# The evidence products of the first pair: from halves of 64 contexts two at a time to quarters of 32 contexts four at a time

## The chip, the cores and the metric

The kernel runs on one core of a Trainium2 chip. A core has TensorE for matrix products (PE in the profile, and PEld for its loads of the stationary operand), VectorE (DVE), ScalarE (ACT), GpSimd (POOL) and SyncE (SP, which here issues transfers). The metric is the device time in microseconds of one execution, median of several runs.

## The reference, cut to what matters

Eight sequences of 512 tokens with 256 features. Each token attends to 64 contexts of its sequence, and the result, the evidence, enters every layer that follows beside the normalised token.

```
nx = layer_norm(x)                                # (8, 512, 256)
scores = (nx @ Wq) @ (prototype_bank @ Wk).T * H ** -0.5
weights = softmax(scores)                         # over 64 contexts
evidence = weights @ (prototype_bank @ Wv)
combined = concat([nx, evidence, anchor])         # (8, 512, 768)
h = silu(combined @ e_w1 + e_b1)                  # three experts of 512
expert_out = h @ e_w2 + e_b2
routed = sum(expert_out * router_probs)           # over the experts
g = sigmoid(silu(combined @ gate_w1 + gate_b1) @ gate_w2 + gate_b2)
out = x + g * (routed @ out_w + out_b)
```

## The kernel before, in words

The sequences are taken in four pairs, j = 0 to 3, all in fp32. Features lie on the 128 partitions and the 512 tokens of one sequence along the free dimension. The evidence itself is never formed. The context values are multiplied by the weights first (`S["vw", j]`, one half of 64 partitions for each sequence of the pair), and a layer adds the product of these values (stationary, 64 partitions by 128 columns) with the softmax weights (`S["wT", j]`, moving, 64 partitions by 512 tokens) to what the nx products of that layer left in a bank of PSUM. These are the evidence products. In the trace and in the order they read `<-wT,vw`.

The first layer works on chunks of 128 output features, two chunks to a group. Group 0 is the gate, groups 1 to 6 are the three experts with two groups each. In one group seven nx products, in a scheme that saves the eighth, go to three banks: U, Y and Z (`U[n]`, `Y[n]`, `Z[n]`, tiles ps_u, ps_y, ps_z). Between products, ACT copies the bank (`keep_part`) and DVE adds the later ones (`add`, L1074 to L1076). A bank is used again by the next group, with the tile framework's semaphores keeping order. For the first pair (j = 0) the order of PE's work is that of the calls in `gate_layer` and `expert_layer`. Each engine takes its instructions in the order of the program.

For the first pair there are four blocks of evidence products, all from the function `evidence`:

- block 1, at the end of `gate_layer`: eight products, for Y0, Z0, U0 and a fourth bank W of group 0, and for the fresh banks Y and Z of groups 1 and 2;
- blocks 2 and 3, at the ends of the first and the second expert: eight products each, U and Z of the two groups that are ending, Y and Z of the two groups that follow;
- block 4, at the end of the third expert: four products, U and Z of groups 5 and 6.

Products of the two sequences alternate, so that one uses rows 0 to 63 of TensorE's array and the next rows 64 to 127. A product appears in the trace as two matmul records and two weight loads, called passes here.

After block 1 DVE adds Y0, Z0 and W to what was kept, then makes `T` (fourth combination of the pair's x, L675), which the product U0 of the next layer reads as its moving operand. After block 2 ACT applies two silus to U1 and U2, copies a weight sum (`v_F`, L909), and computes two standard deviations of the next pair (L584). DVE takes their reciprocals (L590), normalises x of the next pair in eight instructions (L594), adds Y3, and transposes a block of second-layer weights (L515), which PE multiplies next (`ps_w2o`, L523).

For the later pairs (j = 1 to 3) `half_layers` follows a table of 57 slots written by hand. There every product is made in two halves of 64 rows by `half_product`, two to a slot. When the half before it in the same bank ran on other rows of the array, `half_product` lets TensorE's queue wait on a semaphore until that one has ended. `read_bank` forgets what went before in a bank.

Of the kernel before, what the change touches and what calls it, by code (L numbers as in the profile page):

```python
# [16 lines left out]
def kernel(  # L17
# [52 lines left out]
    P = 128  # L70
    B, T, H = x.shape
    CT = context.shape[1]
# [55 lines left out]
    TB = 32  # L128
# [55 lines left out]
    rows = scr[:, P : 2 * P]  # L184
# [375 lines left out]
    S = {}  # L560
# [256 lines left out]
    def values(j, c=0):  # L817

        return S["vw", j] if j < 2 or c >= NE else w1[:, KH + j - 2, :]
# [190 lines left out]
    def product(ps, lhsT, rhs, start=False):  # L1010

        return nc.tensor.matmul(ps, lhsT, rhs, start=start, stop=True, skip_group_check=not start)  # L1012

    def half_product(ps, lhsT, rhs, half, start=False):

        prior_half, prior = last_half.get(ps.name, (half, None))
        if prior_half == half or start:  # L1020
            ins = product(ps, lhsT, rhs, start)
        else:
            tag = bank_of[ps.name]
            if tag not in finished:
                finished[tag] = [tc.alloc_semaphore(f"half_{tag}"), 0]
            finished[tag][1] += 1
            prior.then_inc(finished[tag][0])
            group = f"half_{tag}_{finished[tag][1]}"
            tc.add_to_no_dep_group(group, prior.ins)
            tc.no_tile_sem_insts.add(prior.ins.name)  # L1030
            nc.tensor.wait_ge(*finished[tag])
            ins = product(ps, lhsT, rhs, start)
            tc.declare_fence(ins.ins, group=group)
        last_half[ps.name] = half, ins

    def read_bank(ps):
        last_half.pop(ps.name, None)
# [6 lines left out]
    def evidence(j, groups, W=None):  # L1044

        todo = []
        for n, new in groups:
            c = 2 * GROUPS[n]  # L1050
            for i, ps in ((0, Y[n] if new else U[n]), (1, Z[n])):
                todo.append((ps, i, c + (i if new else 1 - i), new))
        if W is not None:
            c = 2 * GROUPS[0]
            todo[:0] = [(Y[0], 0, c, False), (Z[0], 1, c, False)]
            todo[4:4] = [(U[0], 0, c + 1, False), (W, 1, c + 1, True)]
        for ps, i, c, start in todo:
            half = slice(i * CT, (i + 1) * CT)
            product(ps, values(j, c)[half, c * P : (c + 1) * P], S["wT", j][half, :], start=start)

    def chunk(n, i, d):
        if n == 0:
# [66 lines left out]
    def gate_layer(j, steps):  # L1129
# [29 lines left out]
        W = bank(1, f"ps_w_{j}")  # L1159
        fresh(j, 0)  # L1160
        evidence(j, [(m, True) for m in PAIRS[0]], W=W)

        add(n, 0, 0, Y[n])
# [15 lines left out]
    def expert_layer(j, e, steps):  # L1179
# [62 lines left out]
        if e + 1 < E:  # L1242
            fresh(j, e + 1)
            evidence(j, [(m, False) for m in (a, b)] + [(m, True) for m in PAIRS[e + 1]])
        else:
            evidence(j, [(m, False) for m in (a, b)])
# [387 lines left out]
    with tc.manual_schedule(engines=None):  # L1634
# [5 lines left out]
        for d in range(2):  # L1640
            half = slice(d * NX // 2, (d + 1) * NX // 2)
# [187 lines left out]
```

## Time and profile before

| | us |
|---|---|
| median of three runs | 455.45 (455.0 to 455.94) |
| the profiled execution | 455.56 |
| its span on the core | 453.7 |
| PE busy | 449.2 |
| DVE busy | 367.2 |
| ACT busy | 216.6 |
| POOL busy | 115.8 |

The span runs from the first to the last instruction of the core; 1.86 us of the profiled execution lie around it. Matmuls are pipelined and their ends are modelled, so two passes in a row overlap in the records. The distance between their starts, not their duration, is the time that a pass takes.

### The profile page before, as it was taken

To read this page: it belongs to the slowest core of one execution; us is meant where nothing else is said; L and a number is where in the kernel's file an instruction comes from. 1 tells how busy PE (TensorE), PEld (TensorE's weight loads), DVE (VectorE), ACT (ScalarE), POOL (GpSimd) and SP (SyncE) were. 2 spreads that over 40 slices of the span, in tenths; PEclk is the share of its full clock that TensorE was granted. 3 is DMA by queue.
4 is the path that set the end of the run, shared out by engine and by line. 5 is a ranking of instruction groups with operands and counts; after the bars stand their busy time and mean duration, and the time that the engine had idled before them with its cause. 6 is when DMAs were issued, how large, how long until landed. Compare 5 with 4: busy or idle time off the path is not lost.

```text
span 453.7 us, 5398 instructions
## 1 busy us (share of the span) xinstructions
PE 449.2 (99%) x1707; PEld 213.4 (47%) x1707; DVE 367.2 (81%) x687; ACT 216.6 (48%) x382; POOL 115.8 (26%) x176
## 2 busy tenths in 40 slices
PE   9999999999999999999999999999999999999996
PEld 8644556444444444444444444444444444444445
DVE  4889989668969999857979999777979838678983
ACT  3445685539332257547440276658240356557000
POOL 6558767531242130000243220000151300000020
PEclk9999999999999999999999999999999999999999
DMA  8999698665641567710203158401103381000014
GB/s 256 382 175 188 110 257 165 103 115 105 57 77 28 117 155 172 139 42 7 43 5 45 26 165 167 65 0 30 24 0 46 47 213 22 0 0 1 0 20 74
DMA packets 122124, 41.34 MB, mean 91 GB/s; under 512 B 106452, under 2 KB 115472, under 8 KB 121584
## 3 DMA queue, kind: packets, MB, share of 16 engines
q1 hardware_dynamic: 117184, 29.25, 32.2%
q0 software_dynamic: 4624, 11.63, 10.8%
q8 instruction: 13, 0.21, 0.2%
q14 instruction: 15, 0.12, 0.1%
q10 hardware_dynamic: 288, 0.13, 0.1%
HBM read 31.23 MB, written 7.39 MB: 85 GB/s over the span
## 4 chain that ended last, share of the span: by engine, by line
PE 99%; DVE 0%; issue 0%
PE ps_u L1012 45%; PE ps_z L1012 20%; PE ps_y L1012 14%; PE ps_gu L1012 3%; PE ps_vc L1012 3%; PE ps_w2o L523 2%; PE ps_vw L806 2%; PE ps_s L684 2%; PE ps_gz L1012 2%; PE ps_tokens L1012 1%; PE ps_v L359 1%; PE ps_m L359 1%; PE ps_gy L1012 1%; PE ps_wake L312 1%; PE ps_kq L373 0%; PE ps_ar L462 0%
## 5 line engine op out<-in xcount | busy, mean ns | idle before, releaser
L1012 PE MATMUL ps_u<-nxT,w 64*128 64x512 f32 (+1 forms) x184 | 87.4, 594 | 0.0
L1127 DVE TENSOR_TENSOR h<-h,pb 128x512 f32<-128x512 f32 x96 | 63.1, 694 | 15.9 <-ACT h L1070 11.0
L1012 PE MATMUL ps_u<-h,w2o 128*128 128x512 f32 x144 | 63.9, 593 | 0.0
L1070 ACT ACTIVATE h<-h,abias 128x512 f32<-128x512 f32 x72 | 49.0, 717 | 26.5 <-DVE h L1076 26.2
L1539 POOL TENSOR_TENSOR yb<-yb,xb 128x512 f32<-128x512 f32 x14 | 20.2, 1443 | 129.2 <-DVE yb L1538 115.0
L1012 PE MATMUL ps_z<-T,ws 64*128 64x512 f32 (+1 forms) x92 | 46.4, 590 | 0.0
L1012 PE MATMUL ps_z<-nxT,ws 64*128 64x512 f32 (+1 forms) x92 | 46.0, 591 | 0.0
L1012 PEld LDWEIGHTS ps_u<-nxT,w 64*128 64x128 f32 (+1 forms) x184 | 32.7, 187 | 27.7 <-issue 22.1
L1012 PE MATMUL ps_y<-nxT,w 64*128 64x512 f32 (+1 forms) x92 | 45.5, 590 | 0.0
L1012 PEld LDWEIGHTS ps_u<-h,w2o 128*128 128x128 f32 x144 | 27.3, 190 | 33.3 <-issue 32.1
L1012 PE MATMUL ps_u<-T,ws 64*128 64x512 f32 (+1 forms) x92 | 42.9, 590 | 0.0
L1012 PE MATMUL ps_u<-T,w 64*128 64x512 f32 (+1 forms) x98 | 42.6, 592 | 0.0
L1012 PE MATMUL ps_z<-h,w2s 128*128 128x512 f32 x96 | 42.5, 592 | 0.0
L1079 ACT COPY h<-ps_u 128x512 f32<-128x512 f32 x48 | 27.8, 580 | 17.4 <-PE ps_u L1012 17.4
L437 POOL DMA_DIRECT2D vrd<-vw x8 | 5.0, 632 | 111.2 <-ACT vw L813 111.2
L1506 DVE TENSOR_TENSOR h<-h,h 128x1024 f32<-128x1024 f32 x24 | 30.7, 1333 | 0.0
L1012 PEld LDWEIGHTS ps_z<-h,w2s 128*128 128x128 f32 x96 | 18.2, 190 | 23.0 <-issue 22.2
L1012 PE MATMUL ps_z<-wT,vw 64*128 64x512 f32 x56 | 27.5, 596 | 0.0
L1076 DVE TENSOR_TENSOR h<-h,ps_u 128x512 f32<-128x512 f32 x24 | 16.1, 684 | 10.3 <-PE ps_u L1012 10.3
L1012 PE MATMUL ps_z<-wT,w 64*128 64x512 f32 x48 | 24.1, 589 | 0.0
L1012 PEld LDWEIGHTS ps_z<-T,ws 64*128 64x128 f32 (+1 forms) x92 | 17.3, 188 | 13.2 <-issue 12.2
L1012 PEld LDWEIGHTS ps_y<-nxT,w 64*128 64x128 f32 (+1 forms) x92 | 17.3, 188 | 13.2 <-issue 12.5
(277 smaller groups left out, 889.7 us busy)
## 6 DMA issues: line engine op xcount, KB each, us to landing
pb<-pd POOLq DMA_DIRECT2D x4, 1536.0 KB, 6.5
xb<-in_x_dram SPq DMA_DIRECT2D x64, 64.0 KB, 2.6
x<-in_x_dram SPq DMA_DIRECT2D x28, 128.0 KB, 3.3
out_dram<-yb SPq DMA_DIRECT2D x56, 64.0 KB, 2.0
w<-in_L_xcond_e_w_dram SPq DMA_DIRECT2D x6, 512.0 KB, 9.4
xd<-x SPq DMA_DIRECT2D x24, 128.0 KB, 2.5
xg<-xd SPq DMA_DIRECT2D x48, 64.0 KB, 2.6
scr_wa<-in_L_xcond_e_w_dram SPq DMA_DIRECT2D x3, 512.0 KB, 17.6
```

Of the source, the lines that this page charges most:

```text
L359: nc.tensor.matmul(part(ps, h), w_sb[:, k, m * P : (m + 1) * P], part(src[:, k, :], h), start=(k == 0 and h == 0), stop=(k == KH - 1), ski ...
L437: nc.gpsimd.dma_start(S["vrd", j][i].rearrange("e c -> c e"), S["vw", j][row_half(i), R0:])
L523: nc.tensor.matmul(ps[:, d * H : (d + 1) * H], w2T[:, k, (i + d) * P : (i + d + 1) * P], ow_sb[:, k, :], start=(k == 0), stop=(k == KH - 1),)
L684: nc.tensor.matmul(ps[side(i, h), g * NH : (g + 1) * NH], mr[:, k, 2 * j + i, g * TB : (g + 1) * TB], S["nxT", 2 * j + i][:, k, h * NH : ( ...
L806: nc.tensor.matmul(ps, vT[:, k, j * 2 * CT : (j + 1) * 2 * CT], w1[:, KH + k, n0:n1], start=(k == 0), stop=(k == KH - 1),)
L1012: return nc.tensor.matmul(ps, lhsT, rhs, start=start, stop=True, skip_group_check=not start)
L1070: nc.scalar.activation(h, h if src is None else src, AF.Silu, bias=abias[:, c, 2 * j + i : 2 * j + i + 1])
L1076: nc.vector.tensor_tensor(h, h, part, ALU.add)
L1079: nc.scalar.copy(chunk(n, i, d), part)
L1127: nc.vector.tensor_tensor(h, h, S["pb", j][:, i, :, 2 * q // RC, :], ALU.mult)
L1506: nc.vector.tensor_tensor(d, p, m, ALU.subtract)
L1539: nc.gpsimd.tensor_tensor(yb, yb, S["xb", 2 * j + row][:, i, :], ALU.add)
```

## The change

`evidence` makes each product in two parts of 32 contexts. The products of the first and of the second sequence are listed apart (`first`, `second`). Two of each are taken together: their four banks get one quarter product each, on rows 0 to 31, 32 to 63, 64 to 95 and 96 to 127 of the array. This is called a quad here. The first round (s = 0) goes over all such fours, and the second round (s = 1) goes over them again with the two quarters of each sequence exchanged, so that each bank gets its other 32 contexts. All go through `half_product`, so a second-round product waits on a semaphore for the first-round product of its bank.

```
-        for ps, i, c, start in todo:
-            half = slice(i * CT, (i + 1) * CT)
-            product(ps, values(j, c)[half, c * P : (c + 1) * P], S["wT", j][half, :], start=start)
+        for ps, *_ in todo:
+            read_bank(ps)
+        first, second = ([t for t in todo if t[1] == i] for i in range(2))
+        turns = [(p, s) for s in range(2) for p in range(0, len(first), 2)]
+        for p, s in turns:
+            four = [side_[p + (r ^ s)] for side_ in (first, second) for r in range(2)]
+            for q, (ps, i, c, start) in enumerate(four):
+                rows = slice(q * TB, (q + 1) * TB)
+                half_product(
+                    ps, values(j, c)[rows, c * P : (c + 1) * P], S["wT", j][rows, :], q,
+                    start and not s,
+                )
```

TensorE's order in block 1 before (`ps_y_1` is the bank Y of group 1, the last number is the tile's; the last two rows are the first products of the next layer):

```order
L1012 MATMUL ps_y_0_407<-wT_380,vw_278 128x512
L1012 MATMUL ps_z_0_406<-wT_380,vw_278 128x512
L1012 MATMUL ps_y_1_431<-wT_380,vw_278 128x512
L1012 MATMUL ps_z_1_432<-wT_380,vw_278 128x512
L1012 MATMUL ps_u_0_405<-wT_380,vw_278 128x512
L1012 MATMUL ps_w_430<-wT_380,vw_278 128x512
L1012 MATMUL ps_y_2_433<-wT_380,vw_278 128x512
L1012 MATMUL ps_z_2_434<-wT_380,vw_278 128x512
L1012 MATMUL ps_u_1_465<-nxT_263,w_95 128x512
L1012 MATMUL ps_u_0_405<-T_322,w_95 128x512
```

Here Y0 and Z0 are complete after the first two products and W after the sixth. The same place in the change, from the last two products of the first round on, with the semaphore that each waits for:

```order
L1012 MATMUL ps_w_430<-wT_380,vw_278 128x512
L1012 MATMUL ps_z_2_434<-wT_380,vw_278 128x512
L1012 MATMUL ps_y_1_431<-wT_380,vw_278 128x512 [waits half_4]
L1012 MATMUL ps_y_0_407<-wT_380,vw_278 128x512 [waits half_3]
L1012 MATMUL ps_z_1_432<-wT_380,vw_278 128x512 [waits half_5]
L1012 MATMUL ps_z_0_406<-wT_380,vw_278 128x512 [waits half_2]
L1012 MATMUL ps_y_2_433<-wT_380,vw_278 128x512 [waits half_6]
L1012 MATMUL ps_u_0_405<-wT_380,vw_278 128x512 [waits half_0]
L1012 MATMUL ps_z_2_434<-wT_380,vw_278 128x512 [waits half_7]
L1012 MATMUL ps_w_430<-wT_380,vw_278 128x512 [waits half_1]
L1012 MATMUL ps_u_1_481<-nxT_263,w_95 128x512 [waits DMAHW6_49,DVE_49]
L1012 MATMUL ps_u_0_405<-T_322,w_95 128x512 [waits DVE_49]
```

Y0 and Z0 are now complete in the third of four quads, W in the fourth, and six quarter products stand ahead of these rows. The order of DVE, ACT and POOL is unchanged.

TensorE's order in block 4 before, from the last nx product on:

```order
L1012 MATMUL ps_u_6_882<-T_322,w_95 128x512 [waits DVE_49]
L1012 MATMUL ps_u_5_879<-wT_380,vw_278 128x512
L1012 MATMUL ps_z_5_859<-wT_380,vw_278 128x512
L1012 MATMUL ps_u_6_882<-wT_380,vw_278 128x512
L1012 MATMUL ps_z_6_861<-wT_380,vw_278 128x512
```

And in the change:

```order
L1012 MATMUL ps_u_5_927<-wT_380,vw_278 128x512
L1012 MATMUL ps_u_6_930<-wT_380,vw_278 128x512
L1012 MATMUL ps_z_5_891<-wT_380,vw_278 128x512
L1012 MATMUL ps_z_6_893<-wT_380,vw_278 128x512
L1012 MATMUL ps_u_6_930<-wT_380,vw_278 128x512 [waits half_1]
L1012 MATMUL ps_u_5_927<-wT_380,vw_278 128x512 [waits half_3]
L1012 MATMUL ps_z_6_893<-wT_380,vw_278 128x512 [waits half_7]
L1012 MATMUL ps_z_5_891<-wT_380,vw_278 128x512 [waits half_5]
```

The second round of this block follows the first at once, with no other quad between them.

## Rows read from the trace of the kernel before

**Rows 1.** The page: the span and each engine's busy time.

```profile
span 453.7 us, 5398 instructions
...
PE 449.2 (99%) x1707; PEld 213.4 (47%) x1707; DVE 367.2 (81%) x687; ACT 216.6 (48%) x382; POOL 115.8 (26%) x176
```

**Rows 2.** The waits of TensorE in the whole span: total us, times, longest.

```profile
PE ps_wake L312 <- PEq L1815: 0.8, 1, 0.8
```

**Rows 3.** Timeline of block 1: start us, us, engine, line, operation, [idle before <-releaser].

```profile
29.95 0.69 PE L1012 MATMUL ps_y<-wT,vw 64*128 64x512 f32 x1
30.06 0.69 DVE L1076 TENSOR_TENSOR hg<-hg,ps_u 128x512 f32<-128x512 f32 x1 [0.21 <-PE ps_u L1012]
30.48 0.59 PE L1012 MATMUL ps_y<-wT,vw 64*128 64x512 f32 x1
31.11 0.69 DVE L1076 TENSOR_TENSOR hg<-hg,ps_y 128x512 f32<-128x512 f32 x1 [0.37 <-PE ps_z L1012]
32.20 0.59 PE L1012 MATMUL ps_u<-wT,vw 64*128 64x512 f32 x1
32.84 0.69 DVE L1076 TENSOR_TENSOR hg<-hg,ps_w 128x512 f32<-128x512 f32 x1 [0.45 <-PE ps_w L1012]
33.06 0.59 PE L1012 MATMUL ps_y<-wT,vw 64*128 64x512 f32 x1
33.45 0.80 DVE L675 TENSOR_TENSOR T<-nxT,T 128x512 f32<-128x512 f32 x1
34.30 0.44 PEld L1012 LDWEIGHTS ps_u<-T,w 128*128 128x128 f32 x2 [0.42 <-DVE T L675]
34.55 1.02 PE L1012 MATMUL ps_u<-T,w 128*128 128x512 f32 x2
35.41 1.02 PE L1012 MATMUL ps_u<-nxT,w 128*128 128x512 f32 x2
```

**Rows 4.** Timeline of block 2 and what follows, all engines.

```profile
54.42 0.69 ACT L1070 ACTIVATE h<-ps_u,abias 128x512 f32<-128x512 f32 x1 [2.18 <-PE ps_z L1012]
55.51 0.59 PE L1012 MATMUL ps_y<-wT,vw 64*128 64x512 f32 x1
55.86 0.61 ACT L909 COPY v_F<-v_F 128x512 f32<-128x512 f32 x1
56.89 1.98 PE L1012 MATMUL ps_u<-nxT,w 128*128 128x512 f32 x4
58.12 0.18 DVE L590 RECIPROCAL rstd<-sd 128x4 f32<-128x4 f32 x1 [1.96 <-ACT sd L584]
60.41 1.66 POOL L842 TENSOR_TENSOR v_a<-vT 128x384 f32<-128x384 f32 x1
60.49 1.74 DVE L594 TENSOR_SCALAR x<-x,mv,rstd 128x256 f32<-128x256 f32 x1
62.35 1.88 DVE L594 TENSOR_SCALAR x<-x,mv,rstd 128x256 f32<-128x256 f32 x4
64.74 1.29 DVE L515 STREAM_TRANSPOSE scr_w2T<-scr_w 128x512 f32<-128x512 f32 x2
66.08 2.89 PEld L523 LDWEIGHTS ps_w2o<-ow_sb,scr_w2T 128*128 128x128 f32 x14 [0.23 <-DVE scr_w2T L515]
```

**Rows 5.** Timeline after block 3, DVE.

```profile
88.24 0.69 DVE L1127 TENSOR_TENSOR h<-h,pb 128x512 f32<-128x512 f32 x1 [1.74 <-ACT h L1070]
```

**Rows 6.** Timeline after block 4, ACT.

```profile
101.99 0.59 ACT L885 COPY vw<-ps_vc 128x512 f32<-128x512 f32 x1 [4.10 <-PE ps_vc L1012]
```

**Rows 7.** Timeline of the first pair's scores, TensorE, and the instruction after them.

```profile
18.75 2.05 PE L684 MATMUL ps_s<-nxT,mr 128*32 128x256 f32 x32
20.48 0.76 PE L462 MATMUL ps_ar<-scr_wa,condT 128*32 128x128 f32 x16
```

**Rows 8.** Timeline of TensorE: first of pair 1's 57 slots, first product behind them.

```profile
157.42 0.69 PE L1012 MATMUL ps_y<-wT,vw 64*128 64x512 f32 x1
206.68 1.12 PE L1012 MATMUL ps_gu<-hg,gw_sb 128*128 128x512 f32 x2
```

## The prediction

> **What bounds the kernel now.** I read the page first. TensorE is busy for 449.2 of 453.7 us, the next engine, DVE, for 81% [rows 1]. Busy time alone proves little where ends are modelled, so I turned to the list of waits: TensorE's matmuls stood still for nothing but 0.8 us at the start [rows 2]. Then I read the timeline around the four blocks for the distance between starts. From 32.20 to 33.06 us lie two passes [rows 3], 0.43 us each, and a full-array product takes the same 0.86 us (34.55 to 35.41, [rows 3]). So TensorE bounds the kernel, nearly without gaps, and whatever holds it up in the first 105 us is lost at the end. Nothing later waits for an idle TensorE that could take the loss up.
>
> The reader should see two more things in these rows. The half-row products already run side by side: the first passes of block 1 start at 29.95 and the last at 33.06 [rows 3], which is seven distances of 0.43 us and a slower first one, so eight steps for the sixteen passes of eight products. The array is full already. And several followers are only just in time: the weight load of U0's product is released by T and starts at 34.30, 0.25 us ahead of a matmul that starts without a gap [rows 3], and the load for `ps_w2o` at 66.08 is 0.23 us late because of DVE's transposes [rows 4].
>
> **What the change does to TensorE itself.** Before, 28 products in pairs make 14 times 2 passes. After, 56 quarter products in quads make 14 times 2 passes again. If four run at once, the passes cost 28 times 0.43 = 12.0 us in both. The gain is nothing. Four row quarters at once are shown nowhere in this trace. The nearest row is the scores, where four products on different columns of the array run at once: 32 records from 18.75 until the next instruction at 20.48 [rows 7], that is 8 quads of 0.216 us for 256 columns, half of 0.43 us. So four tiles at once keep full pace there, and I take full pace here. The bound on the other side, two at a time as before, is 12.0 us more; a milder one, 0.53 us for every quad's pass (a block's first pass now, as worked out below), is 28 times 0.10 = 2.8 us. Entry into a block costs something already. The first pass takes 30.48 - 29.95 = 0.53 us instead of 0.43 [rows 3], and four loads instead of two may add 0 to 0.1 us per block, of which I take nothing.
>
> The Trainium skill, TensorE: Matmul & The Clock Gate, section Measured speedup vs the span model, states 3.07 times, not 4, for four row tiles of 32. By it, as an estimate, a quad's pass would take 4 / 3.07 times 0.43 = 0.56 us, the 28 passes 3.6 us more, and the kernel 462.1 us. No row here shows four row tiles; the scores' four column tiles lose no such share.
>
> **The waits of the second round.** Each second-round product stands behind a semaphore. In blocks 1 to 3 a whole quad (0.86 us) lies between a product and its predecessor. Pair 1 has the same waits: its 57 slots run from 157.42 to 206.68 [rows 8], 49.26 us, against 57 times 0.86 = 49.0. I cost these at nothing, since at least one slot lies between there too. In block 4 nothing lies between. The wait ends only when the predecessor has left the array; its modelled duration is 0.59 us [rows 3], 0.16 beyond the 0.43 at which the next pass would start. With the semaphore and the loads that queue behind it, 0.2 to 0.6 us; I take **0.4 us**. ACT has been idle for 4.10 us until 101.99 [rows 6], so nobody behind block 4 is late.
>
> **Block 1: results come later.** DVE starts an add 0.63 us after the start of the bank's last pass (32.20 to 32.84, and 30.48 to 31.11 [rows 3]). Before, Y0 was ready after the second pass; after, its last pass is the sixth. That is where U0's and W's second pass stands now, at 32.20 [rows 3]. The fifth product in the queue is now U0, which waits for DVE's add of the old U0, 30.06 to 30.75 [rows 3]; the third pass was due at 30.91, so its loads come some 0.1 us late. So Y0's add starts at about 32.93. Z0's add, W's and T follow at the distance of 0.61 us seen from 32.84 to 33.45 [rows 3]: T starts at 34.76 and takes 0.80, until 35.56. The load follows 0.05 us after T (34.25 to 34.30), so U0's product starts at 35.6 instead of 34.55, and after an idle stretch its first pass takes 0.53. The next product starts at 36.57 instead of 35.41: **1.15 us**, between 0.9 (no late loads, no slow first pass) and 1.4. The new order also lets U1's product of the next layer wait for Y0's add, since it takes its bank; that wait lies inside the other one. DVE, ACT and TensorE are from here on late by the same amount, so no second loss follows.
>
> **Block 2: two hand-offs.** Before, U1 was ready after the second pass of the block and U2 after the fourth. After, both end with the sixth pass, at 55.51 [rows 4], so the two silus start at 56.14 instead of 54.42 and end at about 57.5. U3's first product takes U1's bank; the first silu ends at 56.83, about when that product was due (56.89 [rows 4]), so 0 to 0.2 us there. The longer way is through ACT: behind the silus stand the copy at 55.86, a table load and the deviations (sd), for which DVE idles 1.96 us until 58.12 [rows 4]. The copy now starts at 57.4, 1.55 us late, and DVE's reciprocal comes at about 59.7. Behind it stand eight normalisations, the add of Y3, and the two transposes at 64.74, for which `ps_w2o` waits already [rows 4]. There is no slack, so TensorE loses what DVE is late by then. It may make up a part: one normalisation took 1.74 us at 60.49 beside a POOL addition that began at 60.41, while four later ones took 1.88 together [rows 4], 0.47 each. After the shift, the first normalisations meet POOL instead of the third and fourth. If one more slips in ahead of POOL's long addition, DVE recovers 0.5 us; if none, little. **1.4 us**, between 0.9 and 1.7, U3's wait included, as it lies inside the same lateness.
>
> **Block 3.** The same lateness of 1.5 us meets DVE with 1.74 us of idle time until 88.24 [rows 5], and ACT with none of the next pair's deviations. What is left is the bank of U5, again about when it was due: **0.05 us**, 0 to 0.3.
>
> **The sum.** 1.15 + 1.4 + 0.05 + 0.4 = 3.0 us; ends together 2.0 and 4.0. Against the profiled execution (455.56: the span of 453.7 and 1.86 around it) this gives 458.6. The median is 455.45, so I say **458.5 us**, its own range 457.4 to 459.7. About 0.2%, 0.9 us, is what a measurement of this kernel tells from no change.
>
> **The rivals.**
> - *Four at a time don't keep pace.* Quarter products of different rows write to four banks at once, which no row shows; the scores of rows 7 write to one. With two at a time 12.0 us come on top (470.5), with 0.53 us for a pass 2.8 (461.3). For it: no row of this form exists. Against it: scores, and pairs, at full pace. 12%.
> - *The hand-offs are absorbed.* If DVE's order gave U0's T and the transposes in time, only block 4 and scraps of entries remain: 0.4 to 1.5 us, 455.9 to 457. For it only POOL's slow-down of the normalisations, which touches one hand-off of two. 13%.
> - *Faster: a quad's pass is shorter than 0.43 us.* A pass over 512 columns might be bound by the rows that one product uses. At half, 0.215, the four blocks would lose 6.0 us, Y0 would be ready earlier than now's W, and the time would be 450. The point from which it decides is 3.0 us on 28 passes, a pass of 0.32 us. Against it: passes of 64 rows and of 128 rows have the same distance of 0.43 [rows 3]. 5%.
> - *Forecast as summed:* 70%.
>
> **How the numbers follow.** 458.5 is the forecast's own. The range goes from 456.3, which takes in half of the absorbed case, to 462, which takes in the milder form of the first rival (461.3); outside lie some 5% of faster, 6% below 456.3 otherwise and 6% above. Slower: the forecast, the first rival, and a small part of the absorbed case, together 0.86. Within 0.2% (up to 456.4): most of the rest of that case, 0.08. Faster: 0.06.
>
> **What would show it.** In the changed trace: quads whose four records start within some 0.03 us and whose passes are 0.43 us apart; DVE's T at about 34.8, the product that reads it at about 35.6 behind an idle gap of 0.5 to 1 us; the deviations 1.55 us later against block 2, and a gap ahead of `ps_w2o`; a gap of 0.2 to 0.6 between the two rounds of block 4. The prediction is wrong if passes of quads are not 0.43 us, if the semaphore waits cost in blocks 1 to 3 too, or if the gaps at U0 and `ps_w2o` are missing.

## The result and the profile after

The changed kernel takes 458.38 us (median of 4 runs, 457.94 to 459.01) against 455.56 us before (median of 4, 455.0 to 455.94). The ratio is 1.0064 with an interval of [1.0047, 1.0081], so it is 2.8 us slower. The prediction was 458.5 us, in a range of 456.3 to 462. The profiled execution took 459.01 us.

The page of the changed kernel, span and busy times, to be read against [rows 1]:

```profile
span 457.2 us, 5520 instructions
...
PE 450.9 (99%) x1763; PEld 217.2 (48%) x1763; DVE 365.8 (80%) x687; ACT 216.3 (47%) x382; POOL 115.0 (25%) x176
```

TensorE has 56 passes and 56 weight loads more (28 products became 56) and the whole program 122 instructions more. The span grew by 3.5 us, and TensorE's busy time by 1.7. The rest is in new waits, which the list of TensorE's waits names (total us, times, longest; before, only the first row was there [rows 2]):

```profile
PE ps_wake L312 <- PEq L1824: 0.8, 1, 0.8
PE ps_u L1012 <- DVE T L675: 0.7, 1, 0.7
PE ps_u L1012 <- DVE h L1085: 0.5, 1, 0.5
PE ps_w2o L523 <- ACT h L1079: 0.5, 1, 0.5
```

The second row is block 1, the fourth is the stretch behind block 2. The third is neither. It lies in pair 3, and the prediction had nothing there.

Of the 3.5 us, 0.5 lie ahead of block 1, whose first pass stands at 30.46 us instead of 29.95 [rows 3]. Up to there the two kernels have the same code, and in the thirteen profiled executions of this document that pass starts between 29.49 and 30.71 us, so this part is put down to scatter. What follows accounts for the other 2.9 us.

Timeline of block 1 in the changed kernel, the same places as in [rows 3]:

```profile
30.46 0.70 PE L1012 MATMUL ps_y<-wT,vw 32*128 32x512 f32 x2
30.99 0.59 PE L1012 MATMUL ps_y<-wT,vw 32*128 32x512 f32 x2
31.42 0.59 PE L1012 MATMUL ps_u<-wT,vw 32*128 32x512 f32 x1
31.44 0.59 PE L1012 MATMUL ps_z<-wT,vw 32*128 32x512 f32 x1
32.71 0.59 PE L1012 MATMUL ps_y<-wT,vw 32*128 32x512 f32 x2
33.35 0.69 DVE L1085 TENSOR_TENSOR hg<-hg,ps_y 128x512 f32<-128x512 f32 x1 [2.10 <-PE ps_z L1012]
35.15 0.69 DVE L675 TENSOR_TENSOR T<-nxT,T 128x512 f32<-128x512 f32 x1
35.89 1.12 PE L1012 MATMUL ps_u<-T,w 128*128 128x512 f32 x2 [0.66 <-DVE T L675]
36.85 0.59 PE L1012 MATMUL ps_u<-nxT,w 128*128 128x512 f32 x1
```

The records of one quad start within 0.02 us of each other, and the next quad's pass starts 0.43 us later (30.99, 31.42). Four row quarters keep full pace. DVE now idles 2.10 us for Y0's last pass at 32.71 instead of 0.37 [rows 3], T starts at 35.15, and TensorE stands still for 0.66 us ahead of the product that reads it. From the block's first pass to the product behind that one it takes 36.85 - 30.46 = 6.39 us, where it took 35.41 - 29.95 = 5.46 [rows 3]: 0.93 us lost.

Timeline of block 2 and what follows, to be read against [rows 4]. The sixth pass of the block stands at 56.95 here and stood at 55.51 there:

```profile
56.95 0.59 PE L1012 MATMUL ps_u<-wT,vw 32*128 32x512 f32 x2
57.60 1.26 ACT L1079 ACTIVATE h<-ps_u,abias 128x512 f32<-128x512 f32 x2 [3.92 <-PE ps_z L1012]
57.81 0.59 PE L1012 MATMUL ps_y<-wT,vw 32*128 32x512 f32 x2
58.35 1.98 PE L1012 MATMUL ps_u<-nxT,w 128*128 128x512 f32 x4
58.75 0.62 ACT L909 COPY v_F<-v_F 128x512 f32<-128x512 f32 x1
61.01 0.18 DVE L590 RECIPROCAL rstd<-sd 128x4 f32<-128x4 f32 x1 [1.98 <-ACT sd L584]
61.23 3.27 DVE L594 TENSOR_SCALAR x<-x,mv,rstd 128x256 f32<-128x256 f32 x4
61.72 1.63 POOL L842 TENSOR_TENSOR v_a<-vT 128x384 f32<-128x384 f32 x1
64.62 1.67 DVE L594 TENSOR_SCALAR x<-x,mv,rstd 128x256 f32<-128x256 f32 x4
66.81 1.29 DVE L515 STREAM_TRANSPOSE scr_w2T<-scr_w 128x512 f32<-128x512 f32 x2
67.62 0.30 PEld L523 LDWEIGHTS ps_w2o<-ow_sb,scr_w2T 128*128 128x128 f32 x2 [1.25 <-issue]
67.65 3.57 PE L523 MATMUL ps_w2o<-ow_sb,scr_w2T 128*128 128x256 f32 x15 [0.45 <-ACT h L1079]
```

Timeline of the kernel before, with a normalisation that [rows 4] leaves out, one of POOL's two transfer issues beside it, and the first load of `ps_w2o`:

```profile
59.23 0.91 POOL L848 DMA_DIRECT2D v_F<-in_L_xcond_e_w_dram  x1
59.35 1.21 DVE L594 TENSOR_SCALAR x<-x,mv,rstd 128x256 f32<-128x256 f32 x1
...
65.56 0.30 PEld L523 LDWEIGHTS ps_w2o<-ow_sb,scr_w2T 128*128 128x128 f32 x2 [0.64 <-issue]
```

Measured from the block's sixth pass, the copy comes at 1.80 us (before 0.35), the reciprocal at 4.06 (before 2.61), the transposes at 9.86 (before 9.23) and the first load of `ps_w2o` at 10.67 (before 10.05). The hand-off through ACT is 1.45 us late. By the transposes only 0.63 us of it is left, since DVE took 5.80 us from the reciprocal to the transposes where it had taken 6.62. Before, two of its eight normalisations were long: the third took 1.21 us while POOL issued its transfers `v_F` (59.23) and `v_G` (59.82), the fourth 1.74 beside POOL's additions [rows 4]. In the change only one is long, the second with 1.72 us beside the additions.

Timelines behind block 3, first TensorE, then DVE. Block 3's exit, from its last pass to the product behind it, takes 87.06 - 86.52 = 0.54 us, and DVE's idle time of 1.74 us [rows 5] has shrunk to 0.26, so it covered the lateness:

```profile
86.52 0.59 PE L1012 MATMUL ps_y<-wT,vw 32*128 32x512 f32 x2
87.06 1.98 PE L1012 MATMUL ps_u<-nxT,w 128*128 128x512 f32 x4
...
90.31 0.69 DVE L1136 TENSOR_TENSOR h<-h,pb 128x512 f32<-128x512 f32 x1 [0.26 <-ACT h L1079]
```

Timeline of block 4. The second round begins at 102.21:

```profile
101.52 0.59 PE L1012 MATMUL ps_u<-wT,vw 32*128 32x512 f32 x2
102.21 0.70 PE L1012 MATMUL ps_u<-wT,vw 32*128 32x512 f32 x2
102.74 0.59 PE L1012 MATMUL ps_u<-wT,vw 32*128 32x512 f32 x2
102.83 0.66 PE L1012 MATMUL ps_z<-wT,vw 32*128 32x512 f32 x2
103.42 1.13 PE L1012 MATMUL ps_vc<-w,v_na 128*128 128x512 f32 x2
```

The step between the rounds is 0.69 us instead of 0.43; the round's first pass takes 0.53; and as Z's records trail U's by 0.09 us, the exit takes 0.68 us against 0.54 behind block 3. Together 0.26 + 0.10 + 0.14 = 0.50 us.

Timeline in pair 3, DVE and TensorE:

```profile
377.24 0.69 DVE L1136 TENSOR_TENSOR h<-h,pb 128x512 f32<-128x512 f32 x1 [5.74 <-DMA pb<-pd]
...
378.58 0.69 PE L1012 MATMUL ps_u<-nxT,w 64*128 64x512 f32 x1 [0.54 <-DVE h L1085]
```

The tile pb, router probabilities spread to all partitions, is moved by POOL's transfer `pb<-pd`. DVE waits for it (4.88 us before, 5.74 here), and now TensorE waits for DVE. The 57 slots of pair 3 take 50.18 us instead of 49.32. Every other stretch behind block 4 (up to pair 1, pairs 1 and 2, between the pairs, behind pair 3) keeps its length within 0.02 us, so the blocks and pair 3 are the whole of the loss.

All runs are laid out in one table. The columns of blocks and of pair 3 are taken from one profiled execution of each kernel: how much longer than before it takes from the first pass of block 1 to that of block 2 (23.31 us before), from there to block 3 (28.08) and on to block 4 (17.57), from block 4's first pass to the product behind it (1.92), and through pair 3's slots (49.32). e1 to e11 are the experiments of the next section.

| kernel | median (before beside it) | ratio | block 1 | block 2 | block 3 | block 4 | pair 3 |
|---|---|---|---|---|---|---|---|
| the change | 458.38 (455.56) | 1.0064 [1.0047, 1.0081] | 0.93 | 0.63 | 0.01 | 0.51 | 0.86 |
| e1, block 1 alone | 456.56 (455.69) | 1.0018 [1.0005, 1.0031] | 1.10 | -0.18 | 0 | 0 | -0.01 |
| e2, block 2 alone | 456.42 (455.69) | 1.0017 [1.0005, 1.0029] | 0 | 0.44 | 0 | 0 | -0.01 |
| e3, block 3 alone | 455.95 (455.69) | 1.0003 [0.9995, 1.0012] | 0 | -0.07 | 0.01 | 0 | 0.31 |
| e4, block 4 alone | 456.20 (455.69) | 1.0007 [0.9998, 1.0017] | 0 | -0.03 | 0 | 0.51 | 0 |
| e5, pairs, late order | 457.46 (455.68) | 1.0040 [1.0027, 1.0052] | 0.92 | 0.72 | 0 | 0 | 0 |
| e6, rounds adjacent | 460.40 (455.68) | 1.0100 [1.0086, 1.0114] | 1.55 | 0.77 | 0.95 | 0.51 | 0.56 |
| e7, hand-offs moved | 457.39 (455.68) | 1.0036 [1.0024, 1.0049] | 0.02 | 0.35 | 0 | 0.52 | 0.81 |
| e8, before, same moves | 456.25 (455.68) | 1.0009 [1.0000, 1.0018] | 0 | 0.34 | 0 | 0 | -0.01 |
| e9, change, more waits | 458.05 (455.81) | 1.0061 [1.0048, 1.0074] | 0.94 | 0.22 | 0 | 0.52 | 0 |
| e10, before, 122 waits | 456.87 (455.81) | 1.0024 [1.0013, 1.0035] | 0 | 0 | -0.01 | 0 | 0.57 |
| e11, before, 56 waits | 455.72 (455.81) | 0.9998 [0.9989, 1.0007] | 0.24 | -0.09 | 0 | -0.01 | 0 |

Each distance comes from a single execution. The code of the blocks is that of before in e10 and e11, so 0.24 and -0.09 in the last row show how far a single distance scatters. The same holds for block 2 of e9, whose code up to there is that of the change (0.22 beside 0.63). What a row adds up to lies within 0.4 us of what its median lies above before, if the added waits of e9 and e10 (0.3 and 0.2 us, below) are counted in. Outside these columns only e1 and e2 lost something, 0.64 and 0.16 us between block 4 and pair 1; in e1 TensorE waited there 0.5 us for ACT's copy `g_r` (L1487), a wait that no other of these profiles lists, and e1's median doesn't show the loss.

### The profile page after: what moved, and what is told of

It reads as the page before. It is cut to its first block, busy times and chain, and to the rows that moved or that the text cites. A ratio compares the mean times of both kernels' runs of the same rounds, so it can differ in the third digit from the quotient of the medians.

```text
span 457.2 us, 5520 instructions
## 1 busy us (share of the span) xinstructions
PE 450.9 (99%) x1763; PEld 217.2 (48%) x1763; DVE 365.8 (80%) x687; ACT 216.3 (47%) x382; POOL 115.0 (25%) x176
## 4 chain that ended last, share of the span: by engine, by line
PE 88%; DVE 7%; DMA 2%; issue 1%; ACT 1%; POOL 0%; DVEq 0%; POOLq 0%
PE ps_u L1012 39%; PE ps_z L1012 17%; PE ps_y L1012 12%; PE ps_gu L1012 3%; PE ps_vc L1012 3%; PE ps_w2o L523 2%; DMA pb<-pd 2%; PE ps_vw L806 2%; PE ps_s L684 2%; PE ps_gz L1012 2%; PE ps_tokens L1012 1%; DVE h L1515 1%; DVE x L594 1%; PE ps_v L359 1%; PE ps_m L359 1%
## 5 line engine op out<-in xcount | busy, mean ns | idle before, releaser
L1012 PE MATMUL ps_z<-wT,vw 32*128 32x512 f32 (+1 forms) x82 | 28.5, 600 | 0.0
```

## The experiments

**One block at a time (e1 to e4).** The quads stay in one block, the other three keep pairs. The block's number is the edit:

```
+        block = 1 if W is not None else 4 if len(todo) == 4 else 2 if groups[0][0] in PAIRS[0] else 3
+        if block not in (1,):
+            for ps, i, c, start in todo:
+                half = slice(i * CT, (i + 1) * CT)
+                product(ps, values(j, c)[half, c * P : (c + 1) * P], S["wT", j][half, :], start=start)
+            return
         for ps, *_ in todo:
```

Expected of e1: 

> Quads in block 1 alone, pairs as before in blocks 2 to 4. Theory (late hand-offs: passes of quads keep 0.43 us, the loss is what waits for DVE or ACT behind a block): T starts 1.7 us later against the block's first pass, its reader late by 0.9 us, nothing more anywhere; time 0.9 us over before, 456.5. Rival (the form itself costs, by slower passes or by the semaphores of the second round): a quarter to a third of the whole loss of 2.8 us, 0.7 to 0.95, but as a longer block, with eight passes taking longer than 3.64 us, and not as a gap at T. The time alone does not tell these two apart, the gap does.

Expected of e2: 

> Quads in block 2 alone. Theory: the deviations come 1.5 us later against the block's first pass, the normalisations meet POOL at another point and make up 0.8 us of that, and ps_w2o is late by 0.6 us; time 456.2. Rival (the form itself costs): the block itself is longer by 0.7 us or more and ps_w2o has no wait for DVE that is longer than before.

Expected of e3: 

> Quads in block 3 alone, the same sixteen quarter products and eight semaphore waits as in block 2, but DVE and ACT are idle behind it for longer than they are late. Theory: no loss, 0 to 0.1 us, time as before (455.5). Rival (the form itself costs): 0.7 us or more, 456.2 or later. This is the run that tells quads from hand-offs.

Expected of e4: 

> Quads in block 4 alone, where the second round stands right behind the first. Theory: the second round starts 0.69 us after the last pass of the first instead of 0.43, a slow first pass follows, 0.5 us in all, time 456.0. Rival (the last block costs no more than any other, the loss being the same in each form): the same as the run with block 3 alone.

The medians lie 0.87, 0.73, 0.26 and 0.51 us above before. They add up to 2.4 us, nearly the whole change. In block 3 a quad costs nothing (0.01 us), and that block has eight products in quads like the others. From the first pass to the product behind them, eight products in quads take 3.65 us in e1, e2 and e3, and in pairs 3.63 or 3.64. What blocks 1 and 2 lose is therefore no price of the quads' passes: it stands in the lists of TensorE's waits, 0.8 us ahead of T's reader in e1 and 0.3 ahead of `ps_w2o` in e2. By their times e1 and e2 can be told from no change; e3 and e4 cannot, though e4's profile shows its 0.51 us in place. e3's 0.26 us is more than forecast for it, and its profile has 0.31 us in pair 3, not in block 3.

**Pairs in the late order (e5).** Before, with no quad, but with the products of blocks 1 and 2 sorted so that Y0, Z0 and W, or U1 and U2, are complete about as late as in the change.

```
+        if block == 1:
+            todo = todo[2:4] + todo[6:] + todo[:2] + todo[4:6]
+        if block == 2:
+            todo = todo[4:] + todo[:4]
         for ps, i, c, start in todo:
```

Expected: 

> No quads at all: pairs of 64 rows as before, but in block 1 the pair of Y0 and Z0 stands third and that of U0 and W last, and in block 2 the pairs of Y3, Z3 and Y4, Z4 stand ahead of those of U and Z. Theory (late hand-offs): the same losses without the change's form, 0.9 us at T's reader, and 0.6 to 1.0 us at ps_w2o, since U2 is ready one pair later than with quads; time 457.1 to 457.5. Rival (the form itself costs): as before, 455.5.

It lost 0.92 us in block 1 and 0.72 in block 2, as much as the change. The timeline of TensorE behind its block 1, which began at 30.22, shows the same wait:

```profile
35.63 1.12 PE L1012 MATMUL ps_u<-T,w 128*128 128x512 f32 x2 [0.66 <-DVE T L675]
```

So the order alone is enough to make this loss: a bank that is finished later hands over later.

**Rounds adjacent (e6).** The change, but each four gets its second round at once, with no other quad between.

```
-        turns = [(p, s) for s in range(2) for p in range(0, len(first), 2)]
+        turns = [(p, s) for p in range(0, len(first), 2) for s in range(2)]
```

Expected: 

> All quads, but the second round of each four stands right behind its first, in all blocks. Banks are complete earlier (Y0 after four passes instead of six), and seven times a second round waits for the semaphores of the pass just ahead. Theory (such a wait costs 0.35 to 0.5 us, as in block 4 of the changed kernel): blocks 1 to 3 grow by 0.7 to 1.0 us each, hand-offs then cost 0.3 to 0.5 at T and next to nothing at ps_w2o; time 3.0 to 4.0 us over before, 458.5 to 459.5. Rival (the wait in block 4 is special to that place): blocks 1 to 3 keep their length, and with the earlier banks the time falls to 456.3 to 457.

Timeline of TensorE in the second half of its block 3:

```profile
86.17 0.66 PE L1012 MATMUL ps_y<-wT,vw 32*128 32x512 f32 x2
86.89 0.70 PE L1012 MATMUL ps_y<-wT,vw 32*128 32x512 f32 x2
87.43 0.59 PE L1012 MATMUL ps_y<-wT,vw 32*128 32x512 f32 x2
88.15 1.98 PE L1012 MATMUL ps_u<-nxT,w 128*128 128x512 f32 x4
```

The step into the second round is 0.72 us instead of 0.43, the next one 0.54, the exit 0.72. A block with two such places took 0.95 us longer, 0.48 for each, as in block 4; block 1 and its hand-off lost 1.55 us instead of 0.93. In the change a whole quad lies between the rounds of blocks 1 to 3, and it hides this wait. The time of 460.40 us lies above the forecast of 458.5 to 459.5: T's reader cost 0.60 us beside the longer block 1, where 0.3 to 0.5 stood, and the 0.56 us of pair 3 had not been forecast.

**The two hand-offs moved (e7), and before with the same moves (e8).** DVE makes T ahead of its adds of block 1, and the two deviations of the next pair are taken ahead of block 2's silus, so that neither depends on when a block's banks are complete.

```
+        combine_x(0, nc.vector, (3,))
         add(n, 0, 0, Y[n])
...
-                put(within, (0, "S"), combine_x, 0, nc.vector, (3,))
...
-                        put(within, (1, "S"), deviation, b)
+                        put(within, (0, "E"), deviation, b)
```

Expected of e7: 

> All quads as in the change, but DVE makes T ahead of its adds behind block 1, while it is idle, and ACT makes the two deviations ahead of the silus behind block 2. Theory: T's reader and ps_w2o no longer wait; what is left is block 4's 0.5 us, 0 to 0.1 for U1's product, which waits for Y0's add, and 0 to 0.4 for U3's, which waits for silus that a table load may delay; time 456.0 to 456.5. Rival (the form itself costs): the loss stays at 2.0 us or more, 457.5 or later.

Expected of e8: 

> The kernel before, with pairs, and the same two moves as in the run ahead of this one, as its control and as a candidate. Theory: TensorE had no gap at T, and 0.2 us at ps_w2o; 0 to 0.2 us off, 455.3 to 455.5. Rival (the moves give time by themselves, so that the run ahead shows nothing of the hand-offs): 1 us off or more.

Timeline of TensorE behind block 1 in e7 (first pass of the block at 29.97): the reader of T follows without a gap.

```profile
33.63 1.13 PE L1012 MATMUL ps_u<-nxT,w 128*128 128x512 f32 x2
34.59 1.02 PE L1012 MATMUL ps_u<-T,w 128*128 128x512 f32 x2
35.45 1.02 PE L1012 MATMUL ps_u<-nxT,w 128*128 128x512 f32 x2
```

Block 1's loss falls from 0.93 to 0.02 us, with the quads still there. Block 2 loses 0.35 us in e7 and 0.34 in e8. What is left there is a price of the move, and the quads add nothing to it. The timeline of e8 shows where that price is, in TensorE's wait for a silu behind a table load that the move brings:

```profile
55.84 1.28 ACT L1070 ACT_TABLE_LOAD   x1
57.14 1.26 ACT L1070 ACTIVATE h<-ps_u,abias 128x512 f32<-128x512 f32 x2
57.88 1.98 PE L1012 MATMUL ps_u<-nxT,w 128*128 128x512 f32 x4 [0.45 <-ACT h L1070]
```

e7 is still 1.7 us slower than before: 0.35 and 0.52 in the blocks and 0.81 in pair 3. Its forecast of 456.0 to 456.5 was missed, mostly by pair 3, and by its time alone it could not be told from its rival; the gap at T that is gone decides. e8's forecast of 455.3 to 455.5 was missed too; the wait behind the table load makes 0.34 us of that. No kernel of these runs is faster than the one before beyond what its interval leaves open.

**Pair 3 (e9 to e11).** In the change, e6 and e7 pb lands late (8.6 to 8.9 us from its issue until its data have arrived) and TensorE stands still in pair 3. The view of transfers of the changed kernel, window 375 to 376 us, by queue (packets, MB, share of 16 engines), shows what else happens there:

```profile
q8 instruction: 1, 0.02, 6.4%
```

The view of the tile pb in the same kernel gives the issue and the time to landing:

```profile
L790 POOL DMA_DIRECT2D pb<-pd x1: 552/552/552, 368.3 to 368.3; - x1
...
DMA to landing us min/median/max: 8.8/8.8/8.8
```

A transfer of instructions falls into the last third of pb's landing. In the kernel before, it stood at 381.5 us, and pb (issued at 366.1, 7.6 us to landing) had long arrived. The three kernels shift it by instructions for TensorE alone: waits in pairs 1 and 2 that have already been fulfilled are written two to four times. In e9 this is done to the change, in e10 and e11 to before.

```
-            nc.tensor.wait_ge(*finished[tag])
+            for _ in range(4 if ps.name.split('_')[2] in ('1','2') else 1):
+                nc.tensor.wait_ge(*finished[tag])
```

This is e9. e10 has 4 for the banks U and Y and 3 for Z, e11 has 2.

Expected of e9: 

> The changed kernel, with 142 more instructions on TensorE's sequencer: the semaphore waits of pairs 1 and 2 on the half products are each written four times instead of once; no product, transfer or order is touched. Theory (the stall of TensorE in pair 3 comes from the transfer of instructions that falls inside the landing of the tile pb): the fetch that stood at 375.0 us, inside the landing from 368.3 to 377.1, comes about 10 us earlier, before pb is issued; pb lands in 7.2 to 8.0 us, the 57 slots of pair 3 take 49.3 us instead of 50.18, and the kernel takes about 457.7 us, 2.0 to 2.1 above the kernel before. Rival (the late landing comes from something else that the change did, or is scatter): pair 3 stays at 50.1 to 50.2 and the kernel at about 458.4. A third: the waits themselves cost time in pairs 1 and 2, whose slots would then take longer than before; each by about 0.03 us would make 4 us.

Expected of e10: 

> The kernel before, with 122 more instructions on TensorE's sequencer (waits on half products in pairs 1 and 2 written three or four times), as many as the change adds; no product is changed. Theory: the fetch that stood at 381.5 us comes at about 373, inside the landing of pb (366.1 to 373.7); pb lands in 8.6 to 8.9 us, the 57 slots of pair 3 take 49.9 to 50.2 us instead of 49.32, and the kernel is 0.5 to 0.9 us slower than before (456.2 to 456.6). Rival: no fetch matters; pair 3 at 49.3 and the kernel at 455.7.

Expected of e11: 

> The kernel before, with 56 more instructions on TensorE's sequencer (each of the same waits written twice). The fetch comes at about 377.5 us, earlier than before but after pb has landed. Theory of the fetch: pb lands in 7.2 to 8.0 us, pair 3 at 49.3, the kernel within 0.2 us of before. If the added waits cost time by themselves, the kernel is slower here too, by nearly half of what the same kernel with 122 more shows.

e10, transfers in the window 372 to 373 us:

```profile
q8 instruction: 1, 0.02, 6.9%
```

e10, the tile pb, which was issued at 366.4 us:

```profile
DMA to landing us min/median/max: 8.6/8.6/8.6
```

e10, TensorE in the timeline behind that landing:

```profile
376.47 0.69 PE L1012 MATMUL ps_u<-nxT,w 64*128 64x512 f32 x1 [0.23 <-DVE h L1077]
```

e11, transfers in the window 376 to 377 us:

```profile
q8 instruction: 1, 0.02, 8.7%
```

e11, the tile pb, which was issued at 366.1 us and so had landed at 373.1:

```profile
DMA to landing us min/median/max: 7.0/7.0/7.0
```

With the transfer inside pb's landing (e10) the kernel before gets the late landing and the stall, 0.57 us in pair 3, and is slower by a ratio of 1.0024. With fewer added waits, and the transfer behind the landing (e11), there is neither. e9 is the other way round. There these transfers stand at 358 and 381 us, on either side of the landing (the first was expected some 10 us ahead of the change's 375 and came 17 ahead), pb lands in 7.5 us, and pair 3 takes 49.32 us, as before the change. Since only instructions of TensorE were added, and the transfer moved with them, it is taken here as one of TensorE's own. The Trainium skill, Runtime: NRT & Kernel Launch, section Terms, says that an engine's instruction memory is refilled in blocks of 16 KiB; the 0.02 MB of these rows agree.

Three things don't fit neatly. The waits are not free: pairs 1 and 2 each take 0.17 us longer in e9, together 0.2 in e10. e10 is 1.06 us slower by median, above its forecast of 0.5 to 0.9, and pair 3 with the waits makes 0.8 of that. And e9's times (458.0, 458.01, 458.05, 458.89 and 459.46 us) don't show the gain that its profile shows; with 0.3 us for the waits they can't be told from the change's. So the late landing is shown by three profiles, and its price in time only by e10 against e11.

## Why the prediction was right, and where it was not

**The quads' pace: right.** Passes of 0.43 us with four records within 0.02, and no loss in block 3. The rival with slower quads falls. The 3.07 times of the Trainium skill, TensorE: Matmul & The Clock Gate, section Measured speedup vs the span model, would have made passes of 0.56 us, by the prediction's estimate; the trace differs, 0.43, and the measurement decides. Faster passes (the rival of 450 us) are excluded by the same rows.

**The second round's waits: right.** They cost nothing in blocks 1 to 3 and 0.51 us in block 4, where 0.4 (0.2 to 0.6) stood. e6 shows that the quad between is what hides them: without it each costs 0.48.

**Block 1: right in its path, 0.22 us too large.** T's start was forecast 4.81 us behind the block's first pass and came at 4.69; its reader was forecast at 5.65 and came at 5.43. Two terms were off. The load of U0 did come late, at 31.30 behind DVE's add, but that was still ahead of its pass, which starts at 31.42 in its place; and T took 0.69 us instead of 0.80. e5 and e7 show the path itself: late order without quads makes the loss, and T ahead of the adds removes it.

**Block 2: right in its path, the size wrong.** The step that failed is "It may make up a part", from which I kept 1.4 us of 1.55. The hand-off through ACT was late by 1.45 us, where 1.55 was forecast, but DVE made up 0.82 by the transposes. The forecast looked for a normalisation that slips in ahead of POOL's long addition. What went missing was another one, that of 1.21 us: before, it began beside POOL's two transfer issues and ended 0.15 us after the long addition had begun. In the change the issues begin 0.7 us ahead of the first normalisation instead of 0.9 us behind it. The other profiles agree, but for one. Where DVE began ahead of the issues, one normalisation took 1.20 us (e1, e3, e4, e7, e10, e11), and where it began behind their start, none did (e2, e5, e6, e9). In e8, however, it began 2.4 us ahead, and two beside the issues took 0.41 us each and the next one 2.26. So that POOL is the cause was read from timelines and not tried alone, and how it holds DVE up isn't shown.

The runs with this code lost between 0.22 and 0.63 us, and e2 0.44, so a range that began at 0.9 was too sure of how DVE and POOL would meet. U3's wait was 0: the exit of block 2 takes 58.35 - 57.81 = 0.54 us, as that of block 3. The list of waits puts the gap ahead of `ps_w2o` down to an ACT silu. But its first load started at 67.62, before that silu ended at 67.64, and 0.81 us behind the start of the transposes, as before (0.82); silu and transposes both stand behind the same normalisations. The prediction also misread a row: the load at 66.08 is the third of its group, the first stood at 65.56, and TensorE had no gap there [rows 2]. That there was no slack held all the same.

**Block 3: right.** 0.01 us for 0.05, and DVE's idle time took the lateness.

**Behind block 4: a term was missing.** The prediction said that what holds TensorE up early "is lost at the end", and treated everything behind block 4 as shifted as a whole. Pair 3 lost 0.86 us by pb's landing, and the sum has nothing for it. It is nearly as large as what block 2 was overcharged (0.77): 0.93 + 0.63 + 0.01 + 0.51 + 0.86 = 2.94 us, against a sum of 3.0. That the total was met so closely is luck, two errors of opposite sign. The four blocks alone are 2.08 us, just inside the sum's ends of 2.0 and 4.0. The rival of absorbed hand-offs holds in part: about half of block 2's lateness, nothing of block 1's.

**What stays open.** Why a transfer of 1536 KB lands about 1 us later with one of 16 KB inside its landing isn't shown. Without the small one pb took 7.0 to 8.0 us in this place and with it 8.6 to 8.9; in e3 it took 8.0 with no such transfer inside, and pair 3 lost 0.31 us, in e2 7.9 with no loss, so the slack of pb ends near 8 us. What made the landing so long in e3 isn't shown either.

## What to carry to other kernels

- Where row tiles already fill the array, finer tiles gained no pass here, and taken round by round they finished the first banks later. Look in the profile for who reads the first banks and whether that chain has slack. Here it was the order, not the tile size, that cost 1.6 of 2.9 us.
- A semaphore wait between two tiles of one bank was free here where another quad lay between (blocks 1 to 3), and cost about half a microsecond where none did (block 4, and every block of e6).
- An edit at the start can be paid for at the end. Here a longer instruction stream shifted its own fetches, and one of them met a transfer that had been just in time; so look for waits on transfers that are within a microsecond of being seen.

## What the runs showed of the hardware that was not expected

A transfer of instructions inside the landing of pb, a transfer of 1536 KB, goes with a landing of 8.6 to 8.9 us instead of 7.0 to 8.0. So 122 waits that hold nobody up made a kernel 1.06 us slower by median (e10), of which its profile places 0.57 in pair 3 and 0.2 in pairs 1 and 2. And the same eight normalisations of DVE, with the same addition and waits around them, took 5.80 us instead of 6.62 up to the transposes. A single one takes 0.40 us with no POOL instruction beside it (the last in the change) and 1.72 to 1.74 beside POOL's long additions.
